# Two transformer blocks on one core: heads laid contiguously, rotary halves swapped by a shuffle, attention scores on array quadrants

## The chip, the cores and the metric

The kernel runs on one core of a Trainium2 chip. The metric is device time in microseconds; runs of one kernel are summarised by their median. Engines are named PE (TensorE, with PEld for its weight loads), DVE (VectorE), ACT (ScalarE), POOL (GpSimd) and SP (SyncE, which issues the DMAs). All data are fp32.

## The reference, cut to what matters

Two blocks are computed one after the other on 32 sequences of 64 tokens and 512 features. The first has attention with 8 query heads of 64 features and one shared key and value head, then a gated MLP of width 2048. The second has attention only: 16 query heads of 32 features in 4 groups, each group sharing a key and value head; keys and values come from a latent of 128.

```python
# first block
h = ada_rms(x, time_emb, ln1_w, ln1_tw)
q, k, v = heads(h @ Wq.T), heads(h @ Wk.T), heads(h @ Wv.T)
q, k = apply_rope(q, pos_ids), apply_rope(k, pos_ids)
attn = softmax(q @ k.T / sqrt(64)); ctx = attn @ v
x = x + ctx @ Wo.T
h = ada_rms(x, time_emb, ln2_w, ln2_tw)
x = x + (silu(h @ Wg.T) * (h @ Wu.T)) @ Wd.T
# second block
h = layernorm(x) * (1 + scale) + shift
q = heads(h @ Wq.T); c_kv = h @ Wkd.T
k, v = heads(c_kv @ Wku.T), heads(c_kv @ Wvu.T)
q, k = rope(q), rope(k)          # x * cos + rotate_half(x) * sin
x = x + (softmax(mask(q @ k_exp.T / sqrt(32))) @ v_exp) @ Wo.T
```

`rotate_half` swaps the two halves of a head's features and negates one. A sequence has 64 tokens, and the mask of the second block hides nothing within 64.

## The kernel before, in words

Activations are kept transposed: features on the 128 partitions in four chunks, tokens in columns. The 2048 tokens are cut into 8 units of 256 (four sequences). Three kinds of work exist for a unit: `attention0` (the first block's attention), `mlp` (with a seven-product scheme in place of eight, on sets of weights that SP loads into four rotating buffers) and `attention1` (the second block).

Each is a generator that yields after a piece with two numbers: an estimate of the piece's TensorE time, and of how long the next piece should wait. A small planner, `Order`, picks which generator issues next, and below it a scheduler orders instructions on each engine. So the order of instructions is fixed when the program is built, and changes when the pieces change. While the MLP of unit u runs, `attention0` of unit u+1 and, one or more units behind, `attention1` are woven into it. Before the first MLP stands a head (`attention0` of units 0 and 1) and after the last a tail (what is left of `attention1`, always units 6 and 7). In head and tail a "lean" form of the code is used.

PSUM has eight banks. In the middle, two of them (tag `at`) serve all attention work, two the MLP's first products (`gu`), four its second (`acc`); in head and tail attention may take all.

What the change touches:

- Head layout. Query weights are permuted on the host so that the first halves of several heads lie together on partitions 0 to 63 and the second halves on 64 to 127. For the first block a chunk holds two heads, for the second four heads, one of each key group.
- `rotate` (L493). VectorE multiplies the projection in PSUM by cos (L505, all 128 partitions), then each half of the partitions by sin into the other half (L506, L507, 64 partitions each); GpSimd adds (L508). For the first block's key the same is written out (L589 to L591), and four pieces of 32 partitions are added or copied into `kb` (L607, L610), which holds each key twice: zeros elsewhere make one matmul give the scores of two heads.
- Scores of the first block (L631): for each pair of sequences (t), chunk (c) and sequence of the pair (b), the stationary operand is the chunk's queries, 128 features by 64 tokens, the moving one 128 columns of `kb`. The output of b = 0 goes to PSUM partitions 0 to 63, of b = 1 to 64 to 127, so each uses half of the array's columns. One bank takes one t.
- Scores of the second block (L778): the same with 256 columns, four key groups side by side, made by multiplying the rotated key by a mask of groups (L758 on GpSimd, 1024 columns). Two chunks fill a bank; a bank is a (t, h_).
- `softmax` (L510) on one bank: maximum (L515) and subtraction (L517) on VectorE from PSUM, exponential on ScalarE (L518), sum and reciprocal on VectorE (L520, L521), product on GpSimd (L522). The probabilities are then transposed on TensorE (L528), and multiplied with the values (L647 for the first block, L799 for the second).
- `angles`, `spread`, `sign_of`, `load_mod` (L232) and the buffers of the tail's units follow from the layout.

Of the kernel before, what the change touches and what calls it, by code (L numbers as in the profile page):

```python
# [12 lines left out]
AF = mybir.ActivationFunctionType  # L13
# [37 lines left out]
C_COND, C_VECS, C_CS1, C_MASK, C_FREQ = 0, KC * B, KC * B + 16, KC * B + 16 + 2 * S, KC * B + 20 + 2 * S  # L51
C_ALL = C_FREQ + 1
# [40 lines left out]
def two_blocks(ctx: ExitStack, tc: tile.TileContext, a: dict, out: bass.AP):  # L93
# [38 lines left out]
    for q in range(US):  # L132
        rows = slice(q * HALF0, (q + 1) * HALF0)
        block = ident[rows, rows].unsqueeze(1).to_broadcast([HALF0, 4, HALF0])
        nc.gpsimd.tensor_copy(spread[rows, q].rearrange("p (q f) -> p q f", f=HALF0), block)
    sign_of = fixed("sign_of", [P, 1])
    nc.vector.memset(sign_of[:64], 1.0)
    nc.vector.memset(sign_of[64:], -1.0)
# [13 lines left out]
    freq = small[:, C_FREQ:C_ALL]  # L152

    kblk0 = [fixed(f"kblk0{i}", [P, US, 2, S]) for i in range(2)]
# [75 lines left out]
    def load_mod(i):  # L232

        mods.append([])
        for j, tag in enumerate((("mw", "mw"), ("mw", "mw"), ("h2", "h2"), ("sq", "kb1"))[i]):
            bufs = {"mw": MW, "h2": 2}.get(tag, 1)
            t = work(tag, [P, KC, D // 2], f"mod_{i}_{j}", bufs)
            nc.sync.dma_start(t, a["mod"][i][:, :, j * 256 : (j + 1) * 256])
            mods[i] += [t[:, :, c * P : (c + 1) * P] for c in range(2)]
# [17 lines left out]
    def modulation(i):  # L257
# [3 lines left out]
        for k in range(KC):  # L261
            for c in range(KC):
                nc.tensor.matmul(
                    ps[c * B : (c + 1) * B, :P],
                    condT[:, k, :],
                    mods[i][c][:, k, :],
                    start=(k == 0),
                    stop=(k == KC - 1),
                )
# [17 lines left out]
    def angles(u0):  # L287
# [8 lines left out]
        ang, lo, hi, prod = some("p0", "ang"), some("p0", "lo"), some("pT0", "hi", 512, 1), some("r0", "prod", UT, 1)  # L296
# [113 lines left out]
    RING = {"h": 2, "p": 2, "pT1": 2}  # L410
# [82 lines left out]
    def rotate(dst, src, cos, sin, shape, name):  # L493

        rows = dst.shape[0]
        half = rows // 2
        lo, hi = slice(0, half), slice(half, rows)
        u, v = (work(tag, [P, 512], f"{tag}_{name}") for tag in "uv")

        def cut(t, r):  # L500
            t = t[r, : shape[1] * shape[2]]
            return t.rearrange("p (c t) -> p c t", t=shape[2])

        every = slice(0, rows)
        nc.vector.tensor_tensor(cut(u, every), src[every], cos, ALU.mult)  # L505
        nc.vector.tensor_tensor(cut(v, lo), src[hi], sin[hi], ALU.mult)  # L506
        nc.vector.tensor_tensor(cut(v, hi), src[lo], sin[lo], ALU.mult)  # L507
        nc.gpsimd.tensor_tensor(dst, cut(u, every), cut(v, every), ALU.add)  # L508

    def softmax(sc, scale, name, p):  # L510

        heads = [P, 8, S]
        s3 = sc.rearrange("p (h k) -> p h k", k=S)
        mx = work("mx", [P, 8], f"mx_{name}", 2)
        nc.vector.tensor_reduce(mx, s3, AX.X, ALU.max)  # L515
        p3 = p.rearrange("p (h k) -> p h k", k=S)
        nc.vector.tensor_tensor(p3, s3, mx.unsqueeze(2).to_broadcast(heads), ALU.subtract)  # L517
        nc.scalar.activation(p, p, AF.Exp, scale=scale)  # L518
        sm = work("sm", [P, 8], f"sm_{name}", 2)
        nc.vector.tensor_reduce(sm, p3, AX.X, ALU.add)  # L520
        nc.vector.reciprocal(sm, sm)  # L521
        nc.gpsimd.tensor_tensor(p3, p3, sm.unsqueeze(2).to_broadcast(heads), ALU.mult)  # L522
        return p
# [24 lines left out]
    def attention0(u, room, early=None, late=None):  # L548
# [36 lines left out]

        ku = work("u", [P, 512], f"ku_{u}")[:HD0, :UT]
        kw = work("v", [P, 512], f"kw_{u}")[:HD0, :UT]
        a_, b_ = slice(0, HALF0), slice(HALF0, HD0)
        nc.vector.tensor_tensor(ku, kv[:HD0, :UT], cos[:HD0], ALU.mult)  # L589
        nc.vector.tensor_tensor(kw[a_], kv[b_, :UT], sin[HD0 : HD0 + HALF0], ALU.mult)  # L590
        nc.vector.tensor_tensor(kw[b_], kv[a_, :UT], sin[a_], ALU.mult)  # L591
# [9 lines left out]
        if lean:  # L601
            nc.vector.tensor_tensor(ku, ku, kw, ALU.add)
        for i, part in enumerate((a_, b_)):
            for hh in range(2):
                to = slice((2 * i + hh) * HALF0, (2 * i + hh + 1) * HALF0)
                if lean:
                    nc.scalar.copy(kb[to, :, hh, :], ku[part].rearrange("p (b s) -> p b s", s=S))  # L607
                    continue
                ins = [t[part].rearrange("p (b s) -> p b s", s=S) for t in (ku, kw)]
                nc.vector.tensor_tensor(kb[to, :, hh, :], *ins, ALU.add)  # L610
# [13 lines left out]
        ps = []  # L624
        for t in range(2):
            sc = abank(f"sc0_{u}_{t}")
            for c in range(KC):
                for b in range(2):
                    rows = slice(b * S, (b + 1) * S)
                    cols = slice((2 * t + b) * S, (2 * t + b + 1) * S)  # L630
                    nc.tensor.matmul(  # L631
                        sc[rows, c * P : (c + 1) * P],
                        qT[:, c, cols],
                        kb[:, 2 * t + b].rearrange("p h k -> p (h k)"),
                        start=True,
                        stop=True,
                    )
            ps.append(softmax(sc, HD0**-0.5, f"0_{u}_{t}", space(room, "p", 512, f"p0_{u}_{t}")))
            yield 1.0, (5.0 if "lean" in room else 7.0) * t

        cT = tile4(room, "h", f"cT0_{u}")
        for t in range(2):
            pT = turned(ps[t], f"0_{u}_{t}", space(room, "pT", 512, f"pT0_{u}_{t}")).rearrange("p (c t) -> p c t", c=KC)
# [34 lines left out]
    def attention1(u, room):  # L678
# [76 lines left out]
        kb = space(room, "kb", KC * UT, f"kb1_{u}").rearrange("p (b g s) -> p b g s", b=US, g=NKV1)  # L755
        wide = [P, US, NKV1, S]
# [16 lines left out]
        def scores(t, h_):  # L773
            sc = abank(f"sc1_{u}_{t}_{h_}")
            for j in range(2):
                for b in range(2):
                    cols = slice((2 * t + b) * S, (2 * t + b + 1) * S)
                    nc.tensor.matmul(  # L778
                        sc[b * S : (b + 1) * S, j * 256 : (j + 1) * 256],
                        qT[:, 2 * h_ + j, cols],  # L780
                        kb[:, 2 * t + b].rearrange("p g k -> p (g k)"),
# [3 lines left out]
            name = f"1_{u}_{t}_{h_}"  # L785
            return softmax(sc, HD1**-0.5, name, space(room, "p", 512, f"p{name}"))

        def context(t, ps):
            pTs = []
            for h_ in range(2):  # L790
                name = f"1_{u}_{t}_{h_}"
                pT = turned(ps[h_], name, space(room, "pT", 512, f"pT{name}"))
                pTs.append(pT.rearrange("p (j m t) -> p j m t", j=2, m=2))
                yield 0.5, 1.2 * h_
            cx = abank(f"cx1_{u}_{t}").rearrange("p (b c s) -> p b c s", b=2, c=KC)
# [322 lines left out]
```

## Time and profile before

| | |
|---|---|
| three runs | 1087.56, 1088.15, 1092.83 us; median 1088.15 |
| the profiled execution | 1082.47 us, span 1080.7 us |
| granted TensorE clock, mean | 0.992 of full |
| busy, us | PE 1032.7, PEld 952.6, DVE 573.1, ACT 326.6, POOL 436.5 |
| DMA | 198.48 MB, mean 184 GB/s |
| scores, first block (L631) | 256 records, 16.4 us busy |
| scores, second block (L778) | 256 records, 35.0 us busy |
| contexts, second block (L799) | 256 records, 18.6 us busy |

The span runs from the first to the last instruction of the profiled execution. A fp32 matmul leaves two records, a transpose one. Durations of matmuls overlap in the records, since TensorE pipelines them; what one costs is read from start to next start. An operand is written as, for instance, `128*64 128x256`: contraction rows and output columns of the array that the weights take, then the moving operand.

### The profile page before, as it was taken

How to read it: one execution, taken by the hardware profiler on the slowest of the kernel's cores; microseconds unless marked ns; L12 is line 12 of the kernel's file. 1: busy time of each engine (PE TensorE's matmuls, PEld its weight loads, DVE VectorE, ACT ScalarE, POOL GpSimd, SP SyncE). 2: the span in 40 equal slices, each digit the busy share in tenths (PEclk: the TensorE clock that was granted, in tenths of full speed). 3: DMA queues.
4: the chain of work that ended last, by engine and by line, in shares of the span. 5: the costliest groups of instructions: out<-in, count | busy, mean ns of one | idle time of the engine just before them, and what ended most of it. 6: DMA issues, size and time to landing. Idle time of an engine off the chain costs nothing.

```text
span 1080.7 us, 20647 instructions
## 1 busy us (share of the span) xinstructions
PE 1032.7 (96%) x8154; PEld 952.6 (88%) x8154; DVE 573.1 (53%) x1341; ACT 326.6 (30%) x683; POOL 436.5 (40%) x518
## 2 busy tenths in 40 slices
PE   7888999999999999999999998999999999999898
PEld 6778989989999988998989997998999989999676
DVE  4877556454455568333585249543465354235653
ACT  4431121344214144223333122144323243022422
POOL 4424434534335444235434226334334343244631
PEclk8999999999999999999999999999999999999999
DMA  9617865535655364655555374455556266762001
GB/s 332 234 69 242 288 237 202 190 137 189 235 197 207 118 251 145 214 183 208 183 174 200 125 266 167 131 178 205 214 195 223 105 208 219 269 246 102 2 20 39
DMA packets 68111, 198.48 MB, mean 184 GB/s; under 512 B 7216, under 2 KB 15152, under 8 KB 67504
## 3 DMA queue, kind: packets, MB, share of 16 engines
q1 hardware_dynamic: 68016, 197.17, 51.9%
q8 instruction: 65, 1.06, 0.4%
q14 instruction: 30, 0.25, 0.1%
HBM read 180.37 MB, written 16.78 MB: 182 GB/s over the span
## 4 chain that ended last, share of the span: by engine, by line
PE 73%; DVE 10%; DMA 6%; POOL 3%; ACT 2%; issue 2%; SPq 0%; ACTq 0%; DVEq 0%; POOLq 0%
PE gu L830 29%; PE down L889 15%; PE po L491 9%; PE q L491 8%; DMA set<-sums 3%; DMA set<-in_wmlp 2%; PE sc L778 2%; PE pp L528 1%; PE cx L799 1%; PE lat L491 1%; PE sc L631 1%; PE cx L647 1%; DVE sm L520 1%; PE kv L491 1%; DVE mx L515 1%
## 5 line engine op out<-in xcount | busy, mean ns | idle before, releaser
L830 PE MATMUL gu<-h,set 128*128 128x128 f32 x2048 | 291.8, 278 | 12.4 <-DVE c L849 5.1
L830 PEld LDWEIGHTS gu<-h,set 128*128 128x128 f32 x2048 | 261.3, 193 | 22.6 <-issue 10.1
L830 PE MATMUL gu<-hc,set 128*128 128x128 f32 x1536 | 216.5, 277 | 4.6 <-DMA set<-sums 3.0
L830 PEld LDWEIGHTS gu<-hc,set 128*128 128x128 f32 x1536 | 193.5, 193 | 7.3 <-DMA set<-sums 3.8
L868 POOL TENSOR_TENSOR act<-c,c 128x384 f32<-128x384 f32 x64 | 63.9, 998 | 236.0 <-DVE c L856 159.2
L889 PE MATMUL down<-td,set 128*128 128x128 f32 x1024 | 138.5, 278 | 3.3 <-DMA set<-sums 2.2
L889 PEld LDWEIGHTS down<-td,set 128*128 128x128 f32 x1024 | 126.6, 193 | 5.7 <-issue 3.6
L842 ACT COPY e<-gu 128x128 f32<-128x128 f32 x128 | 33.6, 264 | 271.2 <-PE gu L830 271.1
L889 PE MATMUL down<-act,set 128*128 128x128 f32 x768 | 110.1, 279 | 1.1 <-DMA set<-in_wmlp 1.1
L491 PE MATMUL po<-cT,wo 128*128 128x256 f32 x480 | 109.2, 380 | 1.7 <-ACT cT L656 1.7
L856 DVE TENSOR_TENSOR c<-gu,u 128x256 f32<-128x256 f32 x128 | 53.7, 422 | 107.1 <-PE gu L830 106.0
L889 PEld LDWEIGHTS down<-act,set 128*128 128x128 f32 x768 | 99.0, 193 | 6.8 <-issue 3.5
L844 DVE TENSOR_TENSOR u<-e,gu 128x128 f32<-128x128 f32 x128 | 35.8, 281 | 128.3 <-ACT e L842 128.0
L491 PEld LDWEIGHTS po<-cT,wo 128*128 128x128 f32 x480 | 89.1, 190 | 14.2 <-ACT cT L656 2.4
L522 POOL TENSOR_TENSOR p<-p,sm 128x512 f32<-128x512 f32 x40 | 41.4, 1044 | 100.0 <-DVE sm L521 81.8
L508 POOL TENSOR_TENSOR qT<-u_q,v_q 128x512 f32<-128x512 f32 x30 | 38.3, 1275 | 94.8 <-DVE v_q L507 94.8
L925 ACT ACT_TABLE_LOAD x33 | 42.3, 1283 | 63.7 <-DVE c L856 63.4
L541 DVE TENSOR_TENSOR x<-x,po 128x512 f32<-128x512 f32 x32 | 22.0, 687 | 72.3 <-PE po L491 72.3
L491 PE MATMUL q<-h,wqkv 128*128 128x256 f32 x256 | 58.6, 381 | 0.2 <-ACT r_a L436 0.2
L491 PEld LDWEIGHTS q<-h,wqkv 128*128 128x128 f32 x256 | 47.3, 190 | 6.6 <-ACT r_a L436 0.4
L491 PE MATMUL q<-h,wq 128*128 128x256 f32 x224 | 50.7, 379 | 0.1
L925 ACT ACTIVATE c<-gu 128x128 f32<-128x128 f32 x64 | 17.7, 277 | 108.1 <-DVE c L856 105.6
(272 smaller groups left out, 1473.9 us busy)
## 6 DMA issues: line engine op xcount, KB each, us to landing
set<-sums SPq DMA_DIRECT2D x168, 512.0 KB, 5.6
set<-in_wmlp SPq DMA_DIRECT2D x192, 384.0 KB, 4.7
sums<-set SPq DMA_DIRECT2D x24, 512.0 KB, 3.0
mod<-in_mod SPq DMA_DIRECT2D x8, 512.0 KB, 10.0
x<-in_x SPq DMA_DIRECT2D x8, 512.0 KB, 7.8
out_x<-x SPq DMA_DIRECT2D x16, 256.0 KB, 2.2
a<-in_wmlp SPq DMA_DIRECT2D x24, 128.0 KB, 2.8
wo<-in_wo SPq DMA_DIRECT2D x2, 1024.0 KB, 10.1
```

Source lines behind the costliest of these rows:

```text
L491: nc.tensor.matmul(ps, w[:, k, cols], h[:, k, :], start=(k == 0), stop=(k == KC - 1))
L508: nc.gpsimd.tensor_tensor(dst, cut(u, every), cut(v, every), ALU.add)
L522: nc.gpsimd.tensor_tensor(p3, p3, sm.unsqueeze(2).to_broadcast(heads), ALU.mult)
L541: nc.vector.tensor_tensor(x[:, part], x[:, part], po, ALU.add)
L778: nc.tensor.matmul(sc[b * S : (b + 1) * S, j * 256 : (j + 1) * 256], qT[:, 2 * h_ + j, cols], kb[:, 2 * t + b].rearrange("p g k -> p (g k) ...
L830: nc.tensor.matmul(ps, w[:, slot, k * P : (k + 1) * P], b[of][:, k], start=start and k == 0, stop=k == 1, skip_group_check=True)
L842: nc.scalar.copy(e, ps[:, 0])
L844: nc.vector.tensor_tensor(u2, e, ps[:, 1], ALU.add)
L856: nc.vector.tensor_tensor(c.rearrange("p (a b) t -> p a b t", b=2)[:, :, 1], ps[:, 2:4], u2.unsqueeze(1).to_broadcast([P, 2, HT]), ALU.add,)
L868: nc.gpsimd.tensor_tensor(act[:, 1:4], gate[:, 1:4], c[:, 1:4], ALU.mult)
L889: nc.tensor.matmul(sums_of[u][p][:, c], w[:, slot, c * P : (c + 1) * P], b[of], start=q % NP == 0 and i % 2 == 0 and c == 0, stop=q % NP = ...
L925: nc.scalar.activation(gate[2][:, 0], gate[0][:, 0], AF.Silu)
```

## The change

Heads become contiguous in features. Partitions 0 to 63 of a chunk hold one head of the first block (two of the second), partitions 64 to 127 another. Within a head the rotary halves are arranged so that both partners lie in one group of 32 partitions, 16 apart; VectorE's shuffle swaps them after the product with sin. Scores use 64 rows of the array instead of 128: each half of the partitions has its own matmul and its own PSUM bank, and the first block's matmuls have 64 columns, the second's 128. There are twice as many. `kb` of the first block holds the key twice, once for each half of the partitions, without zeros; the second block's is 512 columns wide. Outside head and tail the first block's softmax takes both t at once. Contexts of the second block (L799) become half as many of twice the columns.

The core of the diff:

```diff
     def rotate(dst, src, cos, sin, shape, name):
-        nc.vector.tensor_tensor(cut(u, every), src[every], cos, ALU.mult)
-        nc.vector.tensor_tensor(cut(v, lo), src[hi], sin[hi], ALU.mult)
-        nc.vector.tensor_tensor(cut(v, hi), src[lo], sin[lo], ALU.mult)
-        nc.gpsimd.tensor_tensor(dst, cut(u, every), cut(v, every), ALU.add)
+        nc.vector.tensor_tensor(v, src, sin, ALU.mult)
+        nc.vector.tensor_tensor(u, src, cos, ALU.mult)
+        nc.vector.stream_shuffle(v, v, OTHER)
+        nc.gpsimd.tensor_tensor(dst, u, v, ALU.add)
 
-    def softmax(sc, scale, name, p):
+    def softmax(banks, scale, name, p):
+        _, heads, r, _ = p.shape
+        for i, sc in enumerate(banks):
+            s3 = sc.rearrange("p (h k) -> p h k", k=S)
+            mx = work("mx", [P, 8], f"mx_{name}_{i}", 2)[:, :heads]
+            nc.vector.tensor_reduce(mx, s3, AX.X, ALU.max)
+            nc.vector.tensor_tensor(p[:, :, i], s3, mx.unsqueeze(2).to_broadcast(wide), ALU.subtract)
+        p3 = p.rearrange("p h r k -> p (h r) k")
+        for n in range(0, heads * r, 8):
+            ...
# attention0, the key
-                nc.vector.tensor_tensor(kb[to, :, hh, :], *ins, ALU.add)
+        nc.vector.tensor_tensor(kb[:HD0], ku, kw, ALU.add)
+        nc.scalar.copy(kb[HD0:], kb[:HD0])
# attention0, the scores
-                    nc.tensor.matmul(
-                        sc[rows, c * P : (c + 1) * P],
-                        qT[:, c, cols],
-                        kb[:, 2 * t + b].rearrange("p h k -> p (h k)"),
-            ps.append(softmax(sc, HD0**-0.5, f"0_{u}_{t}", space(room, "p", 512, f"p0_{u}_{t}")))
-            yield 1.0, (5.0 if "lean" in room else 7.0) * t
+        for ts in ((0,), (1,)) if lean else ((0, 1),):
+            banks = [abank(f"sc0_{u}_{ts[0]}_{r}")[:, : 256 * len(ts)] for r in range(2)]
+            for n in range(KC * len(ts)):
+                t, c = ts[n // KC], n % KC
                 for b in range(2):
+                    for r, sc in enumerate(banks):
+                        of = slice(r * HD0, (r + 1) * HD0)
+                        nc.tensor.matmul(
+                            sc[b * S : (b + 1) * S, n * S : (n + 1) * S],
+                            qT[of, c, cols],
+                            kb[of, 2 * t + b],
+            softmax(banks, HD0**-0.5, f"0_{u}_{ts[0]}", p[:, KC * ts[0] : KC * (ts[-1] + 1)])
+            yield 0.5 * len(ts), 5.0 * ts[0] if lean else 10.0
# attention1, the scores
+            banks = [abank(f"sc1_{u}_{t}_{m}") for m in range(2)]
+            for j in range(4):
                 for b in range(2):
+                    for m, sc in enumerate(banks):
+                        of = slice(m * 64, (m + 1) * 64)
                         nc.tensor.matmul(
-                        sc[b * S : (b + 1) * S, j * 256 : (j + 1) * 256],
-                        qT[:, 2 * h_ + j, cols],
+                            sc[b * S : (b + 1) * S, j * P : (j + 1) * P],
+                            qT[of, j, cols],
+                            kb[of, 2 * t + b].rearrange("p g k -> p (g k)"),
-                yield 1.0, 0.0 if lean and not t else (5.0 if lean else 7.0) * h_
+            yield 0.9, (0.0, 6.0)[t] if lean else 9.0
# buffers and loads
-    kblk0 = [fixed(f"kblk0{i}", [P, US, 2, S]) for i in range(2)]
+    kblk0 = [fixed(f"kblk0{i}", [P, US, S]) for i in range(2)]
-        for z in (kblk0[0], vblk0[0], kblk0[1], vblk0[1], *vblk1):
+        for z in (*vblk0, *vblk1):
-        kb = space(room, "kb", KC * UT, f"kb1_{u}")...
+        kb = space(room, "kb", 2 * UT, f"kb1_{u}")...
```

Besides this, `spread` (which copies angles to partitions) is built from eight smaller copies in place of four; the sign of the sine comes with the small constants in place of two memsets; the fourth modulation's weights go to other buffers and are loaded by three DMAs in place of two; `p` of the first block is one buffer of 1024 columns; the host permutes the weights to match.

## The prediction

> **What bounds the kernel now.** I read the busy shares first, then what TensorE waited for, then TensorE's timeline around the score matmuls, then the head and the tail.
>
> The page's first two parts:
>
> ```profile
> span 1080.7 us, 20647 instructions
> PE 1032.7 (96%) x8154; PEld 952.6 (88%) x8154; DVE 573.1 (53%) x1341; ACT 326.6 (30%) x683; POOL 436.5 (40%) x518
> PE   7888999999999999999999998999999999999898
> ```
>
> TensorE is busy 96% of the span and no other engine passes 53%. Its waits agree: between 72 and 1000 us they add up to 24 us, the longest row being 5.1. So in that stretch a microsecond of TensorE work is a microsecond of time. Head (0 to 72 us) and tail (998 to 1081) are different; their slices show 7 and 8.
>
> What the scores cost is in the timeline (start, length, line, tiles, count; each fp32 matmul leaves two records):
>
> ```profile
> 455.86 0.61 PE L830 MATMUL gu<-h,set 128*128 128x128 f32 x4
> 456.40 1.97 PE L631 MATMUL sc<-kblk,qT 128*64 128x128 f32 x32
> 458.30 0.71 PE L889 MATMUL down<-act,set 128*128 128x128 f32 x4
> ...
> 992.85 1.08 PE L778 MATMUL sc<-kb,qT 128*64 128x256 f32 x8
> 993.86 0.71 PE L889 MATMUL down<-act,set 128*128 128x128 f32 x4
> ...
> 1037.80 3.67 PE L778 MATMUL sc<-own_kb,qT 128*64 128x256 f32 x32
> 1041.40 0.70 PE L740 MATMUL kv<-own_mw,wkv 128*128 128x256 f32 x2
> ```
>
> Start to next start: 4 second-block score matmuls take 1.01 us, 16 take 3.60. The difference gives 0.216 us each; what is left, 0.15, is the switch of array shape. Before the first-block scores, 4 `gu` records take 0.54 where the chain's 16 in 1.79 give 0.45: another 0.09. An excursion into scores costs 0.24 us beside its work. A first-block score takes (1.90 - 0.15) / 16 = 0.109 us. Both are half of what their columns cost on the full array (16 `gu` records in 1.79 us: 0.223 us for 128 columns): the two column halves, one per sequence, already run together.
>
> One line has four tiles:
>
> ```profile
> 65.23 0.65 PE L444 MATMUL qs_b<-sq_b,ones 128*32 128x64 f32 x32 [0.53 <-ACT sq_b L466]
> ```
>
> Its last record lasts 0.22 us, so 31 steps take 0.43 us: 14 ns a record, 28 ns a matmul of 64 columns, a quarter of the full array's 112. Four tiles share the array perfectly, and issue keeps up.
>
> **What the Trainium skill says.** "TensorE: Matmul & The Clock Gate", section Part 3 (Packing small matmuls), says that tiles of different row groups overlap as column tiles do, and that a weight load overlaps matmuls in flight only when its row group differs. The trace agrees for column tiles (14 ns above); no run here shows two row groups at once. "TensorEngine Tiling (Array Packing)", section Tiling Modes, says that a change of mode drains TensorE: here 0.24 us a round trip. Its section Restrictions and Gotchas says that different row tiles must write different PSUM banks, the reason for a bank per half. "SBUF — State Buffer", section Who interferes with whom, says that a VectorE instruction with one SBUF input outside the two-port modes does not contend with GpSimd: it bears on the shuffle; no line here shows one.
>
> **The change part by part.** The order in which the changed kernel's instructions stand on TensorE matters, because a score gains from quadrants only where a matmul of one half is followed by one of the other. In the head and for the second block's units 6 and 7 they alternate. In the middle, of 192 first-block scores (units 2 to 7) 92 alternate and 100 stand in runs of one half (16 and 16, or 10 to 13 and as many); of 192 second-block scores (units 0 to 5) 114 alternate, 78 stand in runs of 5 to 8. A run has only its two column tiles.
>
> - First-block scores, middle: 96 x 0.109 = 10.5 us go. In come 92 x 0.028 = 2.6 and, at half the full rate of 64 columns, 100 x 0.0545 = 5.5. **-2.4.**
> - Second-block scores, middle: 96 x 0.216 = 20.7 go; 114 x 0.054 + 78 x 0.109 = 14.7 come. **-6.0.**
> - Excursions: 40 in all before, 25 after; in the middle 32 to 21, x 0.24: **-2.6**; tail 5 to 2: **-0.7.**
> - Scores of units 6 and 7, tail: 32 x 0.216 = 6.9 to 64 x 0.054 = 3.5: **-3.4.** The head's save 1.7, but there VectorE sets the end (below): 0.
> - Contexts of the second block: half the matmuls of twice the columns, same array time: 0.
> - Rotation: three VectorE instructions stay three (0.69 x 3); the third becomes a shuffle. The page "VectorE: DVE Perf Modes", section The perf-mode tier table, gives about 2400 ns for 2048 elements at one a cycle; less 1536 elements at the page's 0.96 GHz that is an estimated 0.8 us for 512. Bounds 0.42 and 1.5 (L219 with two SBUF inputs runs 0.41 to 1.49 us); I take 0.75. 32 of these add 2 us of VectorE, hidden in the middle behind TensorE's 96%.
> - First-block keys: 24 adds of 0.42 become 6, and 8 ScalarE copies of 0.40 become 8 of whole halves: VectorE -7.5 us, ScalarE +2. Key mask L758: 1024 to 512 columns, GpSimd 1.89 to about 1.04, eight times. All beside other work, but for unit 7's, for which TensorE waited 1.1 us. Fewer memsets, twice the small copies into `spread`, and one more DMA (the fourth modulation's weights in three pieces) lie before work that waits for 9 us of loads: 0.
>
> The order also moves work. Before, unit 5's second block is unfinished when the last `down` ends: 16 transposes (1.8), 2 score groups (1.7), 16 contexts (2.1) and 32 projections (6.9) stand in the tail. After, they stand inside the last MLP. **12.5 us leave the tail and enter the middle.** That alone saves nothing, but it was filler:
>
> ```profile
> PE sc L778 <- ACT r_c L436: 1.7, 1, 1.7
> PE mean L432 <- POOL x L913: 1.6, 1, 1.6
> ```
>
> These are the longest of 6.7 us of waits from 998 us on. Without filler, the root of the norm (table load 1.28, square root 0.31, reciprocal 0.55) stands bare once, and after unit 6's scores VectorE has 4 x (3 x 0.69 + 0.20) + 2.1 + 1.3 = 12.5 us of softmax and rotations against 8.2 us of TensorE work. Against it, the last x update no longer queues behind unit 5's softmax on GpSimd (1.04). I take +3, bounds 0 and +8.
>
> Head: VectorE is packed from 37 to 64 us. Its lean softmax reads two half-filled banks: per unit 4 x (0.42 + 0.42) in place of 2 x (0.69 + 0.68), +0.6, twice; four shuffles +0.2. I take +1.4, bounds -1 (the key copies on ScalarE fall from 1.6 to 0.4 us) and +3.
>
> Sum: middle -11.0 + 12.5, tail -12.5 - 4.1 + 3, head +1.4: **-10.7 us.** The profiled execution took 1082.47 us (span 1080.7 and 1.8 around it), so it would come to 1071.8. The median of the three runs is 1088.15, 5.7 above it; I carry the difference over: 1077.
>
> New waits: a score group now fills both `at` banks, and VectorE frees them after 1.4 and 2.8 us. Behind it on TensorE stands the MLP, then the next user of a bank: by the order 2.2 us of matmuls later at the tightest, mostly 4 to 10. Loads of the MLP's weights land in 5 us with four buffers; a middle 1% shorter hardly strains them (8 us of waits for DMA now). I take 0, bounds -3 and +6.
>
> **The rivals.**
>
> A. Row groups do not overlap (the change does not do on the array what it says). For it: no line shows two row groups together. Against: the 14 ns a record of four tiles. Then alternating scores run at the rate of runs: 92 x 0.027 + 114 x 0.055 + 3.4 = 12 us come back, and the rest sums to +1: 1089.
>
> B. The two banks become the wait: slower. Place: the 18 merged groups of the middle, where the next `at` user stands behind. Price: the second bank's maximum and subtraction, 1.4 us, each time they are not covered, because VectorE is behind with the MLP's additions (three of 0.28, one of 0.42). It decides from 10.7 / 18 = 0.6 us a group; in full, 18 x 1.4 - 10.7 = +14: 1102. Against: 2.2 us of cover at the tightest against 1.4 for the first bank, and VectorE 53% busy.
>
> C. The tail needs no filler (3 us better), the middle's waits shrink with VectorE's and GpSimd's load (3, the bound above) and the head gains at its lower bound (2.4): -19.1, 1069. For it: the tail's longest waits, 1.7 and 1.6, are on engines that unit 5 also occupies. Against: its own chain of latencies, worked out above.
>
> **How the numbers follow.** Forecast as summed (1070 to 1083): 0.57. C: 0.18. A: 0.13. B: 0.12. About 0.5%, 5.4 us, is what a measurement of this kernel can tell from no change. The forecast and C are faster but for a small part of the forecast's upper end: faster 0.74; A and that part: same 0.15; B: slower 0.11. The range 1063 to 1091 takes in C and A; B and a rest below 1063 stay out.
>
> **What would show it.** Right: score groups that alternate with 32 records of 128 columns in about 0.9 us and of 64 columns in 0.45, runs at twice that; TensorE's busy time down by about 15 us; last `down` near 1001, tail about 69 us. Wrong: alternating groups no faster than runs (A); new rows of TensorE waiting for VectorE's maximum or subtraction, above 10 us (B); shuffles over 1.5 us; a head longer than 75 us.

## The result, and the profile after

The changed kernel takes 1085.53 us (median of 20 runs, 1082.81 to 1089.24), the kernel before 1087.57 (20 runs, 1079.43 to 1092.83): a ratio of 0.999, 95% interval 0.9971 to 1.0008. That is no difference that can be measured; the forecast was 1077. Medians are over all executions of a run, while ratios leave out the few slow ones, such as one of 2688 us at the factor 0.82 below. The changed kernel's profiled execution took 1086.17 us (span 1084.1), 0.6 above its median. The profiled execution of the kernel before took 1082.47, 5.1 below its own median over 20 runs. So the two traces differ by +3.7 us where the medians differ by -2.0, and a few us of any difference between them are the luck of two executions.

The first parts of the page after:

```profile
span 1084.1 us, 21449 instructions
...
PE 1026.2 (95%) x8538; PEld 948.3 (87%) x8538; DVE 548.7 (51%) x1377; ACT 322.5 (30%) x681; POOL 434.1 (40%) x520
...
PE   7899899999999989999999998999999999999887
```

TensorE's busy time fell by 6.5 us, not by 15, and its share from 96% to 95%: time that is not busy grew. The timeline (start, length, line, tiles, count) shows that this is not the fault of the scores:

```profile
225.50 1.83 PE L784 MATMUL sc<-kb,qT 64*64 64x128 f32 x32
227.26 0.71 PE L897 MATMUL down<-act,set 128*128 128x128 f32 x4
...
331.53 1.16 PE L633 MATMUL sc<-kblk,qT 64*64 64x64 f32 x64
332.62 0.60 PE L897 MATMUL down<-act,set 128*128 128x128 f32 x3
...
375.31 1.10 PE L784 MATMUL sc<-kb,qT 64*64 64x128 f32 x32
376.35 0.82 PE L897 MATMUL down<-act,set 128*128 128x128 f32 x5
...
1039.67 1.98 PE L784 MATMUL sc<-own_kb,qT 64*64 64x128 f32 x64
1041.58 0.70 PE L743 MATMUL kv<-own_mw,wkv 128*128 128x256 f32 x2
```

The second and third group alternate between the two halves of the partitions: 32 matmuls of 64 columns from start to next start in 1.09 us, 16 of 128 columns in 1.04 (0.15 of each is the switch of shape). The first, at 225.50, is another 16 of 128 columns, but several of one half stand in a row before the other half's turn: 1.76. In the tail 32 matmuls take 1.91 us where half as many, twice as wide, took 3.60 before. Four quadrants share the array.

The windows (start and end of the stage, its length, busy us of each engine with instruction counts, granted clock, DMA share, GB/s) cut each execution at the first `gu` and at the end of the last `down`: head, middle, tail. The first three lines are the kernel before, the next three the changed one; the views are of different runs.

```profile
0.00:71.56 71.56, 58.44 (x516) 47.89 (x517) 46.47 (x99) 30.09 (x67) 29.81 (x45) 0.95 0.65 231
71.56:998.73 927.17, 903.03 (x7132) 848.31 (x7131) 483.61 (x1163) 270.16 (x555) 374.87 (x445) 0.99 0.56 194
998.73:1080.70 81.97, 71.20 (x509) 56.43 (x507) 43.04 (x82) 26.32 (x61) 31.80 (x28) 1.00 0.05 20
```

```profile
0.00:71.29 71.29, 58.63 (x580) 47.61 (x581) 43.07 (x111) 27.71 (x61) 28.99 (x47) 0.93 0.66 232
71.29:1011.03 939.74, 909.02 (x7516) 854.36 (x7515) 470.84 (x1195) 273.68 (x570) 378.22 (x448) 1.00 0.55 192
1011.03:1084.10 73.07, 58.57 (x444) 46.31 (x443) 34.83 (x73) 21.08 (x50) 26.88 (x26) 0.95 0.04 15
```

The head is the same. The middle is 12.6 us longer (forecast: +1.5), the tail 8.9 shorter (forecast: -13.6). The length of a stage less TensorE's busy time, called its **idle time** below, went in the middle from 24.1 to 30.7 us. The waits of TensorE from 71.3 to 1011 us (who waits, for whom, us in total, times, longest):

```profile
PE gu L838 <- DMA set<-in_wmlp: 3.8, 3, 1.8
PE pp L534 <- POOL p L529: 3.8, 3, 2.6
PE down L897 <- DMA set<-in_wmlp: 3.2, 6, 1.0
PE down L897 <- POOL td L879: 1.7, 3, 1.2
PE down L897 <- POOL td L880: 1.1, 2, 0.7
```

In the kernel before, the transposes had waited less:

```profile
PE pp L528 <- POOL p L522: 1.0, 3, 0.4
```

The wait for GpSimd's normalised probabilities `p` went from 1.0 to 3.8 us. All waits of the middle that GpSimd ends sum to 2.1 before and 8.1 now, those that a DMA ends to 8.1 and 10.9; those that VectorE ends fell from 10.1 to 7.0. The tail's longest waits were 1.7 and 1.6 and are now 2.3 and 2.1:

```profile
PE pp L534 <- POOL own_h L529: 2.6, 2, 2.3
PE po L499 <- ACT cT L817: 2.1, 1, 2.1
PE q L499 <- POOL h L713: 1.6, 1, 1.6
PE qs_c L452 <- ACT own_mw L700: 1.3, 1, 1.3
```

### The profile page after: what moved, and what is told of

Its sections match the earlier page's. It is cut to its first block, busy times and chain, and to the rows that moved or that the text cites. A ratio compares the mean times of both kernels' runs of the same rounds, so it can differ in the third digit from the quotient of the medians.

```text
span 1084.1 us, 21449 instructions
## 1 busy us (share of the span) xinstructions
PE 1026.2 (95%) x8538; PEld 948.3 (87%) x8538; DVE 548.7 (51%) x1377; ACT 322.5 (30%) x681; POOL 434.1 (40%) x520
## 4 chain that ended last, share of the span: by engine, by line
PE 69%; DVE 11%; DMA 6%; POOL 5%; issue 2%; ACT 2%; SPq 0%; ACTq 0%; DVEq 0%; POOLq 0%
PE gu L838 27%; PE down L897 14%; PE po L499 10%; PE q L499 8%; DMA set<-in_wmlp 4%; DMA set<-sums 3%; PE pp L534 1%; PE lat L499 1%; PE cx L808 1%; PE sc L784 1%; PE cx L650 1%; DVE mx L519 1%; PE sc L633 1%; DVE sm L527 1%; DVE c L864 1%
## 5 line engine op out<-in xcount | busy, mean ns | idle before, releaser
L838 PEld LDWEIGHTS gu<-h,set 128*128 128x128 f32 x2048 | 261.4, 193 | 19.3 <-issue 11.9
L876 POOL TENSOR_TENSOR act<-c,c 128x384 f32<-128x384 f32 x64 | 66.5, 1040 | 206.8 <-DVE c L864 148.0
L878 POOL TENSOR_TENSOR td<-act 128x256 f32<-128x256 f32 x64 | 47.9, 749 | 9.9 <-DVE act L875 3.6
```

The costliest lines, as they stand in the source:

```text
L838: nc.tensor.matmul(ps, w[:, slot, k * P : (k + 1) * P], b[of][:, k], start=start and k == 0, stop=k == 1, skip_group_check=True)
L876: nc.gpsimd.tensor_tensor(act[:, 1:4], gate[:, 1:4], c[:, 1:4], ALU.mult)
L878: nc.gpsimd.tensor_tensor(td[:, 0:2], act[:, 1:3], act[:, 0:2], ALU.subtract)
```

## The experiments

All times are medians; the kernel before is run beside each and the ratio is to it, so that two runs of different groups are compared best by their ratios (the kernel before itself came out between 1083.8 and 1087.8). The planner of the kernel interleaves the chain of second blocks with the MLPs by `chain = Job(behind(), 0.8 * A1)`; a smaller factor lets the chain come later, and leaves more of unit 5 for the tail. The kernel before and the changed kernel both have 0.8. The factor is the knob of most runs. There are two theories to begin with: **theory 1**, TensorE's saved work is time, and the move of unit 5 out of the tail took it back; **theory 2**, the middle is paced by other things as well, so that work saved on TensorE turns into waits.

**No quadrants, same order** (`e1_full_rows`). Only the rows of the score matmuls change; the sequence of instructions on every engine is that of the changed kernel. Each score then holds the sum over both halves, so the results are not those of the reference.

```
-                        of = slice(r * HD0, (r + 1) * HD0)
+                        of = slice(0, P)
-                        of = slice(m * 64, (m + 1) * 64)
+                        of = slice(0, P)
```

> The changed kernel with every score matmul over all 128 rows instead of over the 64 rows of its half: banks, keys, shuffles and the order on every engine stay, only the row quadrants go (the scores then hold the sum of both halves' products). Work added on TensorE, from the prediction's durations: 92 alternating first-block matmuls of the middle x 0.027 and 114 second-block ones x 0.054, and 64 x 0.054 in the tail: 2.5 + 6.2 + 3.5 = 12.2 us. Theory 1 (TensorE work saved is time saved, and the order of unit 5 took it back): all of it becomes time, 1085.5 + 12 = 1097 to 1098. Theory 2 (the middle is paced by transfers and other engines as well, so work taken from TensorE there turns into waits): the tail's 3.5 and a third or less of the middle's 8.7 become time, 1089 to 1092, and TensorE's waits between 72 and 1000 us fall from 29 us towards the 24 of before.

Measured: 1090.08, ratio 1.0025 (1.0008 to 1.0042): +4.5 us where 12.2 us of work were worked out. The middle and the tail of its windows:

```profile
71.69:1011.57 939.88, 914.12 (x7516) 861.19 (x7515) 471.71 (x1195) 273.69 (x570) 377.89 (x448) 1.00 0.55 192
1011.57:1084.60 73.03, 61.41 (x445) 49.80 (x443) 34.94 (x73) 21.08 (x50) 26.91 (x26) 0.95 0.04 15
```

The scores cost about what was worked out: summed from start to next start, 27.6 us in the middle became 38.0, 4.4 in the tail became 7.4. But the middle's idle time fell to 25.8, and in the tail 3 us more of score work left its length as it was, 73.03 beside 73.07: TensorE's scores are not on the path of that tail. Theory 2's pattern.

The clock has a part in it. The changed kernel's trace has two half-clock stretches of 3.4 us in the middle, this one none, and over all executions the mean granted clock is 0.986 in the changed kernel (20) and 0.992 here (22). In the 42 executions of the kernel before that stand beside this run, the time falls by 8.7 us for 0.01 of clock. By an estimate from these figures some 5 us of what did not come are clock, so that at a like clock most of the added work would have come as time.

**Scores twice** (`e2_twice`): every group issued a second time into the same banks.

```
-            for n in range(KC * len(ts)):
+            for n in 2 * list(range(KC * len(ts))):
-            for j in range(4):
+            for j in 2 * list(range(4)):
```

> The changed kernel with each group of score matmuls issued twice into the same banks (result unchanged), all else alike: a second point on the slope of time against TensorE's score work. Added work: middle 5.6 (first block) + 11.4 (second), tail 3.5, head 1.8 (behind VectorE there): 20.5 to 22 us. Theory 1: 1085.5 + 20 to 22 = 1106 to 1108. Theory 2: tail 3.5 and a third or less of 17: 1089 to 1095.

Measured: 1112.57, ratio 1.0228 (1.0196 to 1.0261): +27 us. The middle grew by 20.7, of which 17.2 are the scores and 2.6 idle time, the tail by 5.5 for 3.5 us of scores, with one more half-clock stretch of 6.8 us there than in the changed kernel. Work added came in full and more, at a mean clock of 0.985; work taken away by the quadrants (the run before this one) came in part. Neither theory alone fits both.

**Unit 5 in the tail** (`a_unit5_in_tail`: 0.72 for 0.8), and **the kernel before with unit 5 in the middle** (`b_unit5_in_middle`: 0.9 for 0.8).

> The changed kernel with the chain of second blocks due at 0.72 of A1 in place of 0.8: unit 5's score groups, transposes, contexts and half of its projections stand after the last down again, as in the kernel before (60.7 us of matmuls after it by the order, 61.6 before, 48.6 in the changed kernel). The order also gives fewer scores in runs (124 in place of 178), 2.6 us less work. Theory 1: the gain reappears: the tail has its filler, waits there fall by 3 to 5: 1078 to 1080, 0.993 of before. Theory 2: where unit 5 stands doesn't matter, the middle's waits swallow it: 1083 to 1086.

> The kernel before with the chain due at 0.9 of A1: no quadrants, but unit 5's second block finished inside the last MLP as in the changed kernel (50.3 us of matmuls after the last down in place of 61.6). Isolates the move from the rest of the change. Theory 1: the kernel before becomes slower by what the change lost, 4 to 8 us: 1092 to 1095. Theory 2: within 2 us of before, 1086 to 1090.

Measured: 1074.70, ratio 0.9881 (0.9848 to 0.9914), and 1091.40, ratio 1.0039 (1.0018 to 1.0061). The gain is there, 12.4 us of it, when unit 5 stays in the tail; the move costs the kernel before 4.3. Middle and tail of the first:

```profile
73.02:987.29 914.27, 888.58 (x7388) 839.36 (x7387) 461.33 (x1176) 259.01 (x551) 373.92 (x443) 1.00 0.57 197
987.29:1070.60 83.31, 70.71 (x572) 55.52 (x571) 44.20 (x93) 29.25 (x64) 31.29 (x30) 0.95 0.05 20
```

With the same work of unit 5 in the tail as before, the middle is 12.9 us shorter than that of the kernel before, 14.5 of it busy time; the scores' part is 11.7 (33.9 to 22.1). Part of the rest is the clock: the kernel before has three half-clock stretches of 3.4 us in its middle, this run none. Middle and tail of the second run, the kernel before with the move alone:

```profile
73.11:1017.37 944.26, 919.49 (x7228) 859.26 (x7227) 486.00 (x1177) 284.76 (x573) 381.81 (x448) 0.99 0.55 192
1017.37:1089.60 72.23, 60.35 (x412) 48.08 (x411) 36.29 (x67) 21.28 (x50) 28.70 (x26) 0.95 0.04 15
```

Beside the kernel before, its middle is 17.1 us longer, 16.5 of it busy time, and its tail 9.7 shorter.

Theory 1 seemed to have won: the tail lacks its filler. The next runs put that to the test, with theory 1a (what stands in the tail decides) against theory 2a (the interleaving of the middle decides). The factors 0.78 and 0.85 give the very tail of the changed kernel, matmul for matmul; 0.75 and 0.70 leave more in it.

> The changed kernel with the chain of second blocks due at 0.78 of A1: the 48.6 us of matmuls after the last down, and their order, are those of the changed kernel; only the places in the middle differ at which second blocks stand among the MLP's matmuls, and fewer scores stand in runs (96 in place of 178: 62 first-block ones x 0.027 + 20 second-block ones x 0.055 = 2.8 us less work). Theory 1a (unit 5 missing as filler of the tail is what took the gain): the tail is as long, so only the 2.8 go: 1082 to 1084. Theory 2a (what took it is this one interleaving of the middle, with stalls of TensorE of 1 to 2.6 us that another interleaving doesn't have): off by more than 4 us from 1083, to either side, with the difference before the last down.

> As the run at 0.78, with the chain due at 0.85 of A1: same tail matmul for matmul, another interleaving of the middle (124 scores in runs in place of 178, 2 us less work). Theory 1a: 1083 to 1085. Theory 2a: off by more than 4 us from 1084, and not like the run at 0.78.

> The changed kernel with the chain due at 0.75 of A1: unit 5's contexts, half of its transposes and its projections stand in the tail (59.4 us of matmuls there), its first score group in the last MLP; 106 scores in runs. Theory 1a: nearly as the run with all of unit 5 in the tail, 1074.7: 1073 to 1077. Theory 2a: anywhere in 1073 to 1088, by its stalls before the last down.

> The changed kernel with the chain due at 0.7 of A1: unit 5's query and key projections stand in the tail too (70.7 us of matmuls after the last down), and next to no scores in runs (32). Theory 1a: filler beyond what the tail's bare latencies need adds nothing or little; work is 2.8 us below the run with unit 5 in the tail (54 first-block scores x 0.027 + 38 second-block ones x 0.055 = 3.5 less, counted against 1074.7): 1070 to 1075. Theory 2a: anywhere in 1070 to 1085.

Measured: 1076.11 (ratio 0.9885, 0.9859 to 0.9911) at 0.78; 1085.25 (0.9984, 0.9968 to 1.0001) at 0.85; 1081.51 (0.993, 0.9909 to 0.995) at 0.75; 1074.79 (0.987, 0.9838 to 0.9902) at 0.70. Theory 1a falls: one and the same tail goes with 1076 and with 1085, in runs made side by side. The middle and tail at 0.78:

```profile
71.20:1003.12 931.92, 906.11 (x7516) 853.30 (x7515) 467.78 (x1195) 268.63 (x566) 373.30 (x448) 0.99 0.57 194
1003.12:1074.50 71.38, 58.20 (x444) 45.88 (x443) 34.83 (x73) 21.11 (x50) 26.87 (x26) 0.95 0.04 15
```

Beside the changed kernel its span is 9.6 us shorter: 4.0 are scores (fewer in runs, 27.6 to 23.6 us), 4.9 are idle time of the middle (30.7 to 25.8), 1.7 are the tail; other terms take 1 back.

**Scores pinned to alternate** (`alt_080`, `alt_070`), **and two more orders of the kernel before** (`b_chain_078`, `b_chain_082`).

```
+                        if n or b or r:
+                            tc.keep_in_program_order(mm)
```

> The changed kernel with its score matmuls pinned one behind the other, so that the two halves alternate in every group: no scores in runs (178 before), excursions into scores 32 in place of 25; the tail is the same matmul for matmul. Work on TensorE: 100 first-block scores x 0.027 + 78 second-block ones x 0.055 = 7.0 less, 7 excursions x 0.24 = 1.7 more: 5.3 us less. Theory 1 (where unit 5 stands is paid once; beyond it TensorE's work is time): 1085.5 - 5.3 = 1080, score time in the middle 22 in place of 27.6. Theory 2 (the interleaving decides, by stalls): off by more than 3 us from 1080 with the score time down all the same, the difference in TensorE's gaps (30.7 us in the middle of the changed kernel) or its half-clock stretches.

> Scores pinned to alternate as above, with the chain due at 0.7 of A1 (70.7 us of matmuls in the tail, same order of the tail as the run at 0.7 without pins; 25 excursions, no runs). Work is 32 x 0.027 = 0.9 us below that run (1074.8). Theory 1: 1074. Theory 2: anywhere in 1068 to 1082.

> The kernel before with the chain due at 0.78 of A1 in place of 0.8: 72.4 us of matmuls after the last down in place of 61.6 (unit 5's projections too), 38 excursions into scores in place of 40. The counterpart of the changed kernel at 0.7. Theory 1: the work is the same, so 1085 to 1089. Theory 2: the old kernel depends on its interleaving as much as the changed one: off by more than 3 us from 1087, to either side.

> The kernel before with the chain due at 0.82 of A1: the tail as before (61.1 us of matmuls), the middle's second blocks a little earlier, 44 excursions in place of 40 (1 us more). The counterpart of the changed kernel at 0.72. Theory 1: 1086 to 1090. Theory 2: off by more than 3 us from 1088.

Measured: 1084.81 (0.9976, 0.9956 to 0.9995) pinned at 0.80; 1077.36 (0.9905, 0.9869 to 0.994) pinned at 0.70, no better than without the pins; the kernel before 1085.11 (0.9996, 0.9976 to 1.0016) at 0.78 and 1103.83 (1.0149, 1.0106 to 1.0192) at 0.82. The pins took 5.5 us of score time out of the middle, as worked out (27.6 to 22.1), and the time fell by 0.7. The waits of the pinned kernel between 69 and 1012 us say where some of it went:

```profile
PE pp L534 <- POOL p L529: 7.3, 6, 2.6
PE down L901 <- DMA set<-in_wmlp: 4.7, 8, 0.9
PE down L901 <- DMA set<-sums: 4.1, 10, 0.7
```

The wait for the probabilities grew from 3.8 to 7.3 us, and the middle's idle time from 30.7 to 33.1. By the traces, GpSimd finished the second half's probabilities mostly 6 to 9 us after the group's last score, with the pins and without, where a group of the kernel before had them mostly after 4 to 7: both banks go through VectorE, ScalarE and GpSimd one behind the other.

So the next runs gave that chain more cover in the plan (`lat5_080`), or took its last step from GpSimd (`dvenorm`). Beside them stand one more order of the kernel before (`b_chain_085`) and a single further execution at 0.82 for its profile (`b_chain_082_look`).

```
-            yield 0.5 * len(ts), 5.0 * ts[0] if lean else 10.0
+            yield 0.5 * len(ts), 5.0 * ts[0] if lean else 15.0
-            yield 0.9, (0.0, 6.0)[t] if lean else 9.0
+            yield 0.9, (0.0, 6.0)[t] if lean else 14.0
```

```
-            nc.gpsimd.tensor_tensor(p8, p8, sm.unsqueeze(2).to_broadcast(wide), ALU.mult)
+            nc.vector.tensor_tensor(p8, p8, sm.unsqueeze(2).to_broadcast(wide), ALU.mult)
```

> The changed kernel with the planner told 5 us more of delay behind a score group (15 and 14 us in place of 10 and 9): the transposes of the probabilities stand further behind the scores, mostly 13 to 16 us of matmuls in place of 6 to 11; same tail, 112 scores in runs in place of 178 (2.9 us less work). Theory 2a (the new wait is that of the transposes for a merged group's softmax): TensorE's wait for GpSimd's p falls from 3.8 us (7.3 with the scores pinned) to below 1.5 and the half-clock stretches behind it go: 1085.5 - 2.9 - 3 - 2 = 1077 to 1079. Theory 2b (stalls only move, other waits take their place; TensorE's gaps in the middle stay at 30 us): 1083 to 1086.

> The changed kernel with the softmax's last multiplication on VectorE in place of GpSimd (40 instructions of about 1 us leave GpSimd, 40 of an estimated 0.7 us, that of VectorE's products of the same size, come to VectorE); almost the same tail, 192 scores in runs. Theory 2a: GpSimd's queue is in the way of p, h and td: TensorE's waits for GpSimd in the middle fall from 8 us to 3 or less, 1080 to 1082. Theory 2b: VectorE's waits (7 us) grow by as much: 1084 to 1088.

> The kernel before with the chain due at 0.85 of A1: unit 5's contexts, transposes and one score group in the middle, its projections in the tail (57.2 us of matmuls there); the counterpart of the changed kernel at 0.75 (1081.5). If the change is worth the forecast's 11 us at equal footing, and orders scatter by some 5 us: 1088 to 1097. If the kernel before is as good at other orders and the change worth nothing: 1075 to 1085.

> A profile of the kernel before at 0.82 of A1, which measured 1103.8. Expected 1098 to 1108. If stalls of the interleaving make the 17 us over the kernel before: TensorE's gaps in the middle at 35 to 40 us in place of 24 and more half-clock stretches there. If it is work: the sum of TensorE's durations 10 us or more above.

Measured: 1085.64 (0.9991, 0.9967 to 1.0015) with the longer cover; 1084.73 (0.9977, 0.9957 to 0.9998) with VectorE's normalisation; the kernel before 1095.66 (1.0097, 1.006 to 1.0133) at 0.85, and 1095.86 in the single execution at 0.82, below the lowest (1098.03) of the six before. With the longer cover the wait for p fell to 1.9 us and the scores to 25.4, but the idle time stayed at 29.9; one wait of 2.7 us is new, for VectorE's angles:

```profile
PE tab L374 <- DVE angle L335: 2.7, 1, 2.7
```

That is theory 2b's pattern: one wait shrinks, others take its place. With VectorE's normalisation the idle time fell to 26.8, but the median by under 1 us. The single execution at 0.82 has 29.7 us of idle time in the middle (24.1 in the kernel before) and, in the whole, about 7 us more of matmul time at a like share of half clock, in small parts over many groups.

**Quadrants off at the better order** (`full_rows_072`: the first edit at 0.72), and VectorE's normalisation there (`dvenorm_072`).

> The changed kernel at 0.72 of A1 (1074.7) with every score matmul over all 128 rows, the order on every engine unchanged (the scores then hold the sum of both halves' products). Work added on TensorE: middle 106 first-block scores x 0.027 + 122 second-block ones x 0.055 = 9.5 us, tail 96 x 0.055 = 5.2 us. If the quadrants' time is the gain and the tail doesn't count (there the same edit at 0.8 changed nothing): 1074.7 + 9.5 = 1084. If half of it disappears in stalls as at 0.8 (4.5 of 12 came): 1078 to 1080. If the gain is the draw of the order: within 2 us of 1074.7.

> The changed kernel at 0.72 of A1 with the softmax's last multiplication on VectorE (138 scores in runs in place of 124). If GpSimd's queue costs here what it cost at 0.8: 1 us below 1074.7, 1072 to 1075. If the interleaving decides anew: 1070 to 1085.

Measured: 1083.29 (0.9992, 0.9972 to 1.0011) and 1076.17 (0.9913, 0.9882 to 0.9944). Without quadrants the order at 0.72 loses 8.6 us, 12 by the ratios (0.9992 beside 0.9881), at the same mean clock (0.991 and 0.990): the gain at that order is the quadrants'. Its middle and tail:

```profile
70.61:997.73 927.12, 901.42 (x7388) 852.34 (x7387) 461.46 (x1176) 259.25 (x551) 374.73 (x443) 1.00 0.56 195
997.73:1084.40 86.67, 75.71 (x572) 61.43 (x571) 44.35 (x93) 29.29 (x64) 31.38 (x30) 0.96 0.05 19
```

The scores add 10.6 us to the middle and the idle time stays where it was, 25.7; and here, with unit 5 as filler, the tail too becomes longer, by 3.4. Taking the normalisation from GpSimd adds nothing.

All orders together, in us:

| order (factor) | kernel before | changed kernel |
|---|---|---|
| 0.70 | | 1074.8 |
| 0.72 | | 1074.7 |
| 0.75 | | 1081.5 |
| 0.78 | 1085.1 | 1076.1 |
| 0.80 | 1087.6 | 1085.5 |
| 0.82 | 1103.8 | |
| 0.85 | 1095.7 | 1085.3 |
| 0.90 | 1091.4 | |
| mean | 1092.7 | 1079.7 |

The changed kernel at 0.70 or 0.72 beats the kernel before by 1.2 to 1.3%, and itself at 0.80 by 1.0%. The two means are over different factors, and the kernel before was not run at 0.70 to 0.75, where the changed kernel is fastest. At the same factor (0.78, 0.80, 0.85) the change is worth 9.0, 2.0 and 10.4 us. Paired by the matmul time that stands after the last `down`, as the expectations give it (0.78 of the kernel before with 0.70, 0.80 with 0.72, 0.85 with 0.75, 0.90 with 0.80), it is worth 10.3, 12.9, 14.2 and 5.9.

## Why the prediction was wrong, point by point

Two steps failed. **New waits in the middle, "I take 0"**: TensorE's idle time there grew by 6.6 us. **Scores of the tail, -4.1**: they gave nothing. Together they are as large as the forecast gain. The sentence under both, that in the middle "a microsecond of TensorE work is a microsecond of time", took the waits of the kernel before, at its order, for those of the changed one.

- **Rates of the quadrants: right.** A matmul of 64 columns takes (1.09 - 0.15) / 32 = 0.029 us alternating, one of 128 columns (1.04 - 0.15) / 16 = 0.056; in runs about 0.10 for 128 columns. The sum of the prediction for the middle's scores, 2.6 + 5.5 + 14.7 with 21 excursions of 0.24, is 27.8; measured 27.6 (which leaves out the 0.09 before each group that the 0.24 holds). Rival A falls.
- **Work saved in the middle, -11.0: right.** From the trace of the kernel before with the same move (`b_unit5_in_middle`) to that of the changed kernel, TensorE's busy time in the middle falls by 10.5 us.
- **Shuffle: right.** 0.727 us for 512 columns (0.75 taken), 0.440 for 256. From the Trainium skill's page "VectorE: DVE Perf Modes", section The perf-mode tier table, the prediction had estimated 0.8; the trace is a little lower.
- **Head: within its bounds.** 71.29 beside 71.56, +1.4 forecast. Heads of the changed kernel's variants lie between 68.8 and 74.1, so one pair of profiles does not settle it.
- **Scores of the tail, -4.1: failed.** Nothing came. With unit 5 gone, TensorE is not what the tail waits for: 3 us more of score work there changed nothing (`e1_full_rows`), and the tail is as long as that of the kernel before with the move alone, 73.07 beside 72.23. The prediction had written down its own evidence, 12.5 us of softmax and rotations against 8.2 of TensorE work, and still subtracted the saving from the longer chain's cover.
- **Filler, +3: right for the tail, though not only by the bare waits.** In the kernel before with the move alone the tail gets 9.7 us shorter, where -12.5 + 3 were forecast. Its idle time grows by 1.1 (10.8 to 11.9); the rest is likely the clock. In both kernels with unit 5 in the middle, this one and the changed one, a stretch of 6.8 us at half clock follows the stalls at the root of the norm (at 1020 us in the changed one, shown below); the profiled execution of the kernel before has none in its tail.
- **New waits in the middle, 0 with bounds -3 and +6: failed**, and the largest term. The idle time grew by 6.6, in the trace by the waits that GpSimd (+6.0) and the DMAs (+2.8) end, while those for VectorE fell (-3.1). Rival B named waits, but the wrong link: not VectorE's maximum and subtraction, for which TensorE hardly waits. That the merged groups are the reason is not shown: the longer way to `p` makes up 2.8 of the 6.6, and GpSimd ends 8.8 to 10.3 us of waits in the kernel before too, at 0.78, 0.82 and 0.85. Rival C falls as well: waits grew, and the tail gained less than forecast.
- **"Alone saves nothing": mis-sized.** The move was costed by its work, and by the tail, at +3 in sum. In the kernel before it costs 4.3 us (2.0 to 6.6), within reach of that, but its work shows in the middle as 16.5 us of busy time in place of 12.5. In the changed kernel it costs 1.4 at 0.78, 10.6 at 0.85 and 10.8 at 0.80, beside 0.72. The prediction counted the order's runs and excursions and took the rest of it as equal.
- **The clock was left out.** The changed kernel's mean clock of 0.986 lies below that of the kernel before, 0.989 to 0.991 in five groups of executions beside the later runs (beside the changed kernel itself it is not on record). By 8.7 us for 0.01 this is an estimated 2 to 4 us. It is not a cause apart from the waits: half-clock stretches follow stalls (last section).

What holds is that the quadrants save about the work that was forecast, and that this work can become time: at 0.72 they are worth 8.6 to 12 us at an unchanged order, and in every pairing above the changed kernel is the faster one, by 2 (not clear of noise) to 14 us. That the forecast of 10.7 lies inside is in part luck, since the order moves either kernel by as much. The medians at the order that both were given differ by 2.0 because 0.80 is the second best of five orders for the kernel before and at the bad end of six for the changed one. That the order decides is shown by runs with the same tail (0.78 beside 0.80 and 0.85), 9 us apart. **Open** stays what makes an order good. Scores in runs account for part (4.0 of 9.6 us between 0.80 and 0.78), single stalls for part, yet removing either by itself (`alt_080`, `lat5_080`, `dvenorm`) gave under 1 us. Nor is it the idle time alone: at 0.70 the middle idles 32.9 us, more than at 0.80, and yet that order is among the fastest; TensorE is busy 1016.4 us there beside 1026.2. Carrying single placements of the order at 0.78 over to 0.80 was not tried.

## What to carry to other kernels

Where a planner or scheduler reorders, a change of about one per cent is measured together with a new draw of the order: give both kernels several orders, the same ones where possible, before judging the change, and expect a scatter as large as its effect. A cut in the busiest engine's work is time only where no other engine's result is waited for instead; test it by giving the work back at an unchanged order, as the two full-row runs did, and compare the granted clocks before the times. And merging two groups to save work lengthens the chain behind the merged one (here from mostly 4 to 7 us to mostly 6 to 9): price the wait of its last consumer too, not only that of its first.

## What the runs showed of the hardware

**Half-clock stretches follow stalls well short of a whole window.** The Trainium skill's page "TensorE: Matmul & The Clock Gate", section What's actually happening, describes a free-running window of 3413 ns and half clock after at least one idle window. The traces agree on the window: between the head and the last microseconds of a span, the half-clock stretches last 3.41 or 6.83 us. They do not agree that it must be idle throughout. Laid over TensorE's idle time in 19 profiled executions, 62 half-clock stretches began there, each after a window with 1.31 to 3.41 us idle. Every full-clock window with more than 1.84 us idle was followed by one; between 1.31 and 1.84 it was 21 times so and some 90 times not; below 1.31 never. So a stall of 2 us can cost, by an estimate (half of 3.41), up to another 1.7 us, by where it falls in the window, and twice that when the stretch lasts 6.83. In the changed kernel's tail (timeline, then windows, where the clock stands ahead of the last two numbers):

```profile
1017.35 0.30 PE L452 MATMUL qs_c<-own_mw,ones 128*32 128x64 f32 x2 [1.35 <-ACT own_mw L700]
1017.58 1.10 PE L374 MATMUL row_c<-r_c,spread 128*128 128x64 f32 x8
1018.62 0.65 PE L452 MATMUL qs_c<-own_mw,ones 128*32 128x64 f32 x30
1020.85 2.07 PE L499 MATMUL q<-h,wq 128*128 128x256 f32 x4 [1.59 <-POOL h L713]
1022.72 1.59 PE L374 MATMUL row_c<-own_mw,spread 128*128 128x64 f32 x7
```

```profile
1013.00:1020.30 7.30, 4.49 (x80) 3.52 (x80) 4.33 (x8) 4.29 (x7) 4.68 (x4) 1.00 0.00 1
1020.30:1027.10 6.80, 6.25 (x19) 5.35 (x20) 1.52 (x3) 0.00 (x0) 3.20 (x4) 0.50 0.00 0
```

Eight `row_c` records take 1.1 us at full clock, seven take 1.6 at half.

**The order of the row halves matters.** Sixteen matmuls that alternate between the row halves of the array take 1.04 us, sixteen of the same shape in runs of one half 1.76.
